# Maxima ahead of the scores in masked attention steps, by quarters of the array, with cleared queries for rows that see no key

## The chip, the cores and the metric

The kernel runs on one core of a Trainium2 chip. The metric is the device time of one execution in microseconds (us), as the median of several runs. PE is the core's matrix engine (TensorE), PEld its weight loads, DVE the vector engine, ACT the scalar engine, POOL is GpSimd, and SP the engine whose queue issues nearly all DMAs. PSUM is the memory that PE's matmuls write, SBUF the other on-chip memory.

## The reference, cut to what matters

Two transformer layers are computed on 2048 rows of width 256, with 16 heads of width 16. The first layer holds a self attention and a cross attention between the two halves of the rows, the second a masked self attention and a cross attention to 1601 context rows; each layer ends in an MLP. That makes four attention stages, numbered 0 to 3 in the kernel. Stage 2 is the masked one:

```python
scores = jnp.einsum('bhqd,bhkd->bhqk', q, k) / jnp.sqrt(jnp.float32(hd))
if mask is not None:
    scores = jnp.where(mask == 0, jnp.float32(-1000000000.0), scores)
attn = jax.nn.softmax(scores, axis=-1)
out = jnp.einsum('bhqk,bhkd->bhqd', attn, v)
```

The mask is a full 2048 by 2048 array of integers, the same for all heads, and the kernel must take any such array. In a row whose keys are all masked, all scores are the same number, so that the softmax is even over all keys.

## The kernel before

**Units and steps.** The rows are worked on in four blocks of 512 queries (`BLK`), the heads in four groups of four (`g`). A unit is one stage, one block and one group. Within a unit a step handles 128 keys for two heads (`i` picks the pair, `h` the head within it): a PSUM tile `s_ps` of 128 keys by 2 x 512 queries. The keys of a stage lie in two slots of 1024. The first masked block (`SPLIT`) is worked on one slot at a time, as part 0 and part 1, because the keys of the second slot are ready later: its eight units have 16 steps. The other three masked blocks have twelve units of 32 steps. That makes 512 masked steps.

**What a step does.** `weights_of` makes the exponentials of one step (PE to PSUM, then one ACT instruction, L1251), transposed, with keys on partitions. In masked stages four matmuls of 64 by 64 first bring in the mask (L1224: an identity times a transposed part of the mask, `bias_columns`, 0 or -2^60). Each takes one quarter of the array: 64 rows (partitions read) by 64 columns (partitions written). Then come two matmuls of scores (L1241, fp32 operands of 64 rows by 128 columns, one for each head), and last two matmuls that subtract each query's maximum (`less_maxima`, L1232, bf16: `sel` holds ones in the rows of `nm` that belong to the head). In unmasked stages the maxima come first and the scores last. A step also does one tile of the next unit's maxima: `maxima` computes scores the other way round (L1142, and L1136 where a head's keys are written in two halves), and DVE reduces them (L1149 for masked tiles, which adds the mask from `bias_rows` too; L1156 for others). And it does a step of the value product of the unit, `values_of` (L1268, four column groups of 32).

**How maxima travel.** When the last tile of a unit's maxima is issued, four steps before the unit's own first step, `all_maxima` calls `negated` (L1170, L1173: three DVE instructions split each negated maximum into three bf16 parts in `maxpad`), and three steps later `as_rows` turns them with four matmuls (L1182) and an ACT copy (L1187) into the rows `nm`. Where a unit is a part, `as_rows` also sends rows of `nm` through twelve DMAs (L1194), by which the two parts are joined later.

**The mask.** `mask_rows` loads 128 queries by 512 keys of the mask (L1043, tile `raw`, two buffers) and POOL turns them into 0 or -2^60 in bf16 (L1044). For the second to fourth masked block this happens while the maxima of the group before (`g` = 3 of the block before) are computed, and `mask_columns` transposes them on PE (L1067) with an ACT copy (L1072).

**What sets the order.** Every engine's instructions stand in the order in which the Python code issues them. `stream` walks through the steps; lists of work with due steps (`later`), generators of background work (projections, norms, the next stage's keys and queries; L113 is their matmuls' line, L404 to L413 a norm) and a list of DMAs (`transfers`) are drawn on at each step. The three `s_ps` buffers are handed round between maxima tiles and exponential tiles; a query tile `q` has three buffers and is loaded two units ahead (L1010). POOL also scales each unit's output by its inverse sums (`divide`, L1344), which waits for a DMA.

Of the kernel before, what the change touches and what calls it, by code (L numbers as in the profile page):

```python
# [22 lines left out]
P = 128  # L23
# [7 lines left out]
BLK = 512  # L31
NB = S // BLK
TPB = BLK // P
# [3 lines left out]
MASKED = -float(2**60)  # L37
# [3 lines left out]
NPART = 3  # L41
# [6 lines left out]
SLOT = S // 2  # L48
# [6 lines left out]
SPLIT = ORDER[2][0]  # L55
# [3 lines left out]
AHEAD = 4  # L59
SPACING = 0.75  # L60
COLUMNS = 6


def key_rows(st, n):
# [3 lines left out]
def slot_rows(st, slot):  # L68
    return sum(key_rows(st, n) for n in KEYS[st][slot])
# [8 lines left out]
def two_layers(ctx: ExitStack, tc: tile.TileContext, a: dict, out: bass.AP):  # L78
    nc = tc.nc

    def pool(name, bufs=1, **kw):
        return ctx.enter_context(tc.tile_pool(name=name, bufs=bufs, **kw))
# [7 lines left out]
    sb = pool("sb")  # L90
# [24 lines left out]
    def big_ps(dtype=F32):  # L115
        flush((None,))
        return ps.tile([P, 2, BLK], dtype, tag="s", bufs=3, name="s_ps")

    def one_ps(dtype=F32, n=None):
        n = small[0] if n is None else n  # L120
        flush((n,))
        return ps.tile([P, BLK], dtype, tag=f"m{n}", bufs=1, name=f"m{n}_ps")
# [37 lines left out]
    ident = identR.bitcast(F32)  # L160
    ident16 = sb.tile([P, P], BF16, tag="ident16", name="ident16")
# [1 line left out]
    minus_half = sb.tile([P, TPB], F32, tag="minus_half", name="minus_half")  # L163
    nc.gpsimd.memset(minus_half, -0.5)

    maxpad = sb.tile([P, TPB, P], F32, tag="maxpad", name="maxpad")
    nc.gpsimd.memset(maxpad, 0.0)

    def upper(t):

        return t.bitcast(BF16).rearrange("... (x two) -> ... x two", two=2)[..., 1]

    sel = sb.tile([P, 2, P], BF16, tag="sel", name="sel")
    for i in range(2):
        col = sb.tile([P, 1], F32, tag=f"col{i}", name="col")
        v = ident.rearrange("p (c x) -> p c x", c=2)[:, :, i : 2 * NPART : 2]
        nc.vector.tensor_reduce(col, v, AX.XY, ALU.add)
        nc.vector.tensor_copy(sel[:, i, :], col.to_broadcast([P, P]))

    kT: list = [[None, None] for _ in range(NG)]  # L180
    V: list = [[None, None] for _ in range(NG)]
# [19 lines left out]
    def half(shape, dtype=F32, name="half"):  # L201
        return sb.tile(shape, dtype, tag="half", bufs=3, name=name)
# [822 lines left out]
    def mask_rows(b, slot, qt, j):  # L1025

        if (b, slot, qt) not in bias_rows:
            if b != SPLIT:
                t = sb.tile([P, 2, SLOT], BF16, tag="w_mlp", bufs=WB, name="bias")
                for s in range(2):  # L1030
                    bias_rows[b, s, qt] = t[:, s, :]
            elif slot == 0:

                t = sb.tile([P, TPB, SLOT], BF16, tag="kT11", name="bias")
                for q in range(TPB):
                    bias_rows[b, slot, q] = t[:, q, :]
            else:
                t = sb.tile([P, 2, SLOT], BF16, tag="w_mlp", bufs=WB, name="bias")
                for q2 in range(2):
                    bias_rows[b, slot, qt + q2] = t[:, q2, :]  # L1040
        raw = sb.tile([P, BLK], I32, tag="raw", bufs=2, name="raw")
        q0, k0 = b * BLK + qt * P, KEYS[2][slot][j] * BLK
        nc.sync.dma_start(raw, a["mask"][q0 : q0 + P, k0 : k0 + BLK])  # L1043
        nc.gpsimd.tensor_scalar(  # L1044
            bias_rows[b, slot, qt][:, j * BLK : (j + 1) * BLK], raw, 0.0, MASKED,
            ALU.is_equal, ALU.mult,
        )

    def mask_part(slot):

        for n in range(2 * TPB):
            later.append([n, lambda n=n: mask_rows(SPLIT, slot, n // 2, n % 2), False])
# [112 lines left out]

    def negated(u):

        v = maxpad.rearrange("p t (c x) -> p t c x", c=2)
        high = upper(maxpad).rearrange("p t (c x) -> p t c x", c=2)
        nc.vector.tensor_reduce(v[:, :, :, :2], u["pm"], AX.X, ALU.max, negate=True)  # L1170
        for n in range(NPART - 1):
            at = slice(2 * n, 2 * n + 2)
            nc.vector.tensor_tensor(  # L1173
                v[:, :, :, 2 * n + 2 : 2 * n + 4], v[:, :, :, at], high[:, :, :, at], ALU.subtract
            )

    def as_rows(u):

        m = one_ps()
        high = upper(maxpad)  # L1180
        for qt in range(TPB):
            nc.tensor.matmul(  # L1182
                m[:, qt * P : (qt + 1) * P], lhsT=high[:, qt, :], rhs=ident16,
                start=True, stop=True,
            )
        u["nm"] = sb.tile([P, BLK], BF16, tag="nm", bufs=2, name="nm")
        nc.scalar.copy(u["nm"], m)  # L1187
        if "part" in u:

            t = sb.tile([P, NPART, 4 * BLK // P], BF16, tag="mh", bufs=2, name="mh")  # L1190
            for j in range(4):
                for h in range(NPART):
                    r = 64 * (j // 2) + 2 * h + j % 2
                    nc.sync.dma_start(  # L1194
                        t[PH * j : PH * (j + 1), h, :], u["nm"][r : r + 1, :]
                    )

            def add():
                n = u["minus"] = part_tile(u, "minus")
                nc.vector.tensor_tensor(n, t[:, 0, :], t[:, 1, :], ALU.add)  # L1200
                for h in range(2, NPART):
                    nc.vector.tensor_tensor(n, n, t[:, h, :], ALU.add)

            later.append([4, add, False])

    def part_tile(u, name):
        return sb.tile([P, 4 * BLK // P], F32, tag=f"{name}{u['g']}{u['part']}", name=name)

    def weights_of(u):

        st, b, g = u["st"], u["b"], u["g"]
        masked = st == 2
        u["tiles"] = [
            (slot, kt, min(P, slot_rows(st, slot) - kt * P))
            for slot in u["slots"] for kt in range(-(-slot_rows(st, slot) // P))
        ]
        u["e"] = {}

        def pair(n, i):
            slot, kt, r = u["tiles"][n]  # L1220
            s = big_ps()
            for h, half_ in ((0, 0), (0, 1), (1, 0), (1, 1)) if masked else ():
                to, of = 64 * half_, 64 * (half_ ^ h)
                nc.tensor.matmul(  # L1224
                    s[to : to + 64, h, :],
                    lhsT=ident16[of : of + 64, of : of + 64],
                    rhs=bias_columns[b, slot, kt][of : of + 64, :],
                    start=True, stop=False,
                )
            def less_maxima():  # L1230
                for h in range(2):
                    nc.tensor.matmul(  # L1232
                        s[:r, h, :],
                        lhsT=sel[64 * h : 64 * h + 64, i, :r],
                        rhs=u["nm"][64 * h : 64 * h + 64, :],
                        start=not masked, stop=masked,
                    )

            def scores():
                for h in range(2):  # L1240
                    nc.tensor.matmul(  # L1241
                        s[:r, h, :],
                        lhsT=kT[g][slot][64 * h : 64 * h + 64, i, kt * P : kt * P + r],
                        rhs=u["q"][64 * h : 64 * h + 64, i, :],
                        start=False, stop=not masked,
                    )

            for f in (scores, less_maxima) if masked else (less_maxima, scores):
                f()
            e = u["e"][n, i] = sb.tile([P, 2, BLK], F32, tag="e", bufs=EB, name="e")  # L1250
            nc.scalar.activation(e[:r], s[:r], AF.Exp, scale=SCALE)  # L1251

        return [lambda n=n, i=i: pair(n, i) for n in range(len(u["tiles"])) for i in range(2)]
# [157 lines left out]
    def stream(stages, start_up):  # L1411
# [19 lines left out]
        at = 0  # L1431
        for u in units:
            steps = [(slot, kt) for slot in u["slots"] for kt in range(-(-slot_rows(u["st"], slot) // P))]
            if u["st"] == 2 and u["g"] == 0:
                columns += [
                    (at + 2 * n - COLUMNS, u["b"], slot, kt) for n, (slot, kt) in enumerate(steps)
                ]
# [20 lines left out]
                    all_maxima(u)  # L1458

        def all_maxima(u):  # L1460
            negated(u)
            later.append([3, lambda: as_rows(u), True])
            if u.get("part") == 0 and u["g"] == NG - 1:
                want(2, 1, 1)
# [38 lines left out]
        for u in units:  # L1503
            i = u["i"]
            masked = u["st"] == 2
            small[0] = i % 2
            second = weights_of(u)
            for s2 in range(len(second)):
# [10 lines left out]
                f = pending.pop(0) if pending else None  # L1519
# [12 lines left out]
                if s2 == 2 and i:  # L1532
# [6 lines left out]
                    elif part == 1:  # L1539
                        v = units[i - 1 - NG]  # L1540
# [143 lines left out]
```

## Time and profile before

| what | value |
|---|---|
| median of 3 runs | 3057.54 us (3054.51 to 3059.77) |
| the profiled execution's own time | 3064.13 us |
| its span in the profile | 3062.4 us |
| mean granted PE clock | 0.971 |
| busy: PE, DVE, ACT, POOL | 2826.0, 2174.5, 1721.8, 388.9 us |
| first to last mask matmul (L1224) | 1129.3 to 2266.9 us |
| L1251, the exponentials | 1440 of 1024 ns |
| L1149, the masked maxima | 1024 of 700 ns |

Times in the profile are of one execution. Each row of a view gives a line of the kernel, its engine, the operation, `out<-in` by the program's names, and the shape; for matmuls a shape such as 64*128 says how many rows and columns of the array it takes. In the timeline instructions of one kind that follow each other are one row; its first number is the start, its second the length. What stands in brackets is how long the engine was idle before the row and what ended that; `issue` there means that no other engine was waited for. The ends of matmuls are modelled, so that two starts tell more than a length. The chain of waits is followed back from the last instruction; its shares say which line's work stood on the path that set the end.

### The profile page before, as it was taken

How to read it: one execution, taken by the hardware profiler on the slowest of the kernel's cores; microseconds unless marked ns; L12 is line 12 of the kernel's file. 1: busy time of each engine (PE TensorE's matmuls, PEld its weight loads, DVE VectorE, ACT ScalarE, POOL GpSimd, SP SyncE). 2: the span in 40 equal slices, each digit the busy share in tenths (PEclk: the TensorE clock that was granted, in tenths of full speed). 3: DMA queues.
4: the chain of work that ended last, by engine and by line, in shares of the span. 5: the costliest groups of instructions: out<-in, count | busy, mean ns of one | idle time of the engine just before them, and what ended most of it. 6: DMA issues, size and time to landing. Idle time of an engine off the chain costs nothing.

```text
span 3062.4 us, 71795 instructions
## 1 busy us (share of the span) xinstructions
PE 2826.0 (92%) x30040; PEld 1258.6 (41%) x30040; DVE 2174.5 (71%) x3856; ACT 1721.8 (56%) x1897; POOL 388.9 (13%) x333
## 2 busy tenths in 40 slices
PE   6999999989998999786999999999999999999997
PEld 2334433333343344333444444444434444444442
DVE  5777777766766577465878878877768858858562
ACT  1466666665655556343555565565556746657472
POOL 0001101101010210203212101301001011110110
PEclk8999999999999999898999999999999999999998
DMA  7652262261205321443212001102242000100000
GB/s 220 143 97 92 67 109 66 75 115 34 73 28 110 60 78 42 108 92 104 68 31 65 29 21 53 55 19 60 46 68 84 24 21 27 28 21 23 21 22 12
DMA packets 178640, 192.11 MB, mean 63 GB/s; under 512 B 95476, under 2 KB 112380, under 8 KB 178316
## 3 DMA queue, kind: packets, MB, share of 16 engines
q1 hardware_dynamic: 177164, 187.52, 24.7%
q8 instruction: 236, 3.87, 0.6%
q14 instruction: 88, 0.72, 0.1%
q10 hardware_dynamic: 1152, 0.00, 0.0%
HBM read 129.78 MB, written 48.45 MB: 58 GB/s over the span
## 4 chain that ended last, share of the span: by engine, by line
PE 73%; DVE 9%; DMA 8%; SPq 4%; ACT 3%; issue 2%; POOL 1%; DVEq 0%; ACTq 0%; POOLq 0%
PE m_ps L1268 20%; PE m_ps L113 12%; PE s_ps L1241 11%; PE s_ps L1232 11%; PE s_ps L1142 8%; PE s_ps L1224 5%; DVE pm L1156 3%; DVE s_ps L1149 2%; PE s_ps L1136 2%; ACT e L1251 1%; DMA rd_dr<-rd 1%; DMA kT<-k_dr 1%; PE s_ps L113 1%; SPq L1194 1%; DVE t L413 1%
## 5 line engine op out<-in xcount | busy, mean ns | idle before, releaser
L1251 ACT ACTIVATE e<-s_ps 128x1024 f32<-128x1024 f32 (+1 forms) x1440 | 1474.0, 1024 | 1054.6 <-PE s_ps L1241 570.0
L1156 DVE TENSOR_REDUCE pm<-s_ps 128x2 f32<-128x1024 f32 x896 | 1090.6, 1224 | 315.2 <-PE s_ps L1142 300.3
L1268 PE MATMUL m_ps<-e,V 128*32 128x256 f32 (+1 forms) x11520 | 928.9, 393 | 11.8 <-DVE lo L496 11.6
L1149 DVE CUSTOM_DVE_ANT_0 s_ps<-s_ps,bias 128x512 f32<-128x512 f32 x1024 | 713.2, 700 | 211.2 <-PE s_ps L1136 191.0
L1241 PE MATMUL s_ps<-q,kT 64*128 64x512 f32 (+1 forms) x2880 | 805.5, 555 | 0.0
L1142 PE MATMUL s_ps<-kT,q 64*128 64x512 f32 (+2 forms) x2560 | 689.0, 436 | 45.9 <-DMA kT<-k_dr 19.3
L1232 PE MATMUL s_ps<-nm,sel 64*128 64x512 bf16 (+1 forms) x2880 | 567.9, 391 | 40.7 <-DVE pm L1156 28.9
L1268 PEld LDWEIGHTS m_ps<-e,V 128*32 128x32 f32 (+1 forms) x11520 | 250.2, 109 | 339.6 <-issue 236.1
L1142 PEld LDWEIGHTS s_ps<-kT,q 64*128 64x128 f32 x2560 | 295.9, 190 | 190.2 <-ACT e L1251 124.6
L1232 PEld LDWEIGHTS <-sel 64*128 64x128 bf16 (+1 forms) x2880 | 144.7, 93 | 506.2 <-issue 470.3
L1241 PEld LDWEIGHTS s_ps<-q,kT 64*128 64x128 f32 (+1 forms) x2880 | 281.6, 192 | 117.2 <-issue 117.2
L1136 PE MATMUL s_ps<-kT,q 64*128 64x256 f32 x1024 | 291.2, 366 | 3.5 <-DMA kT<-k_dr 2.7
L1344 POOL TENSOR_TENSOR oT<-oT,rd_rows 64x512 f32<-64x512 f32 x63 | 80.1, 1271 | 1592.3 <-DMA rd_rows<-rd_dr 1304.7
L1224 PE MATMUL s_ps<-biasT,ident 64*64 64x512 bf16 x2048 | 210.8, 402 | 9.8 <-DVE pm L1149 7.9
L1136 PEld LDWEIGHTS s_ps<-kT,q 64*128 64x128 f32 x1024 | 194.3, 193 | 18.2 <-DMA kT<-k_dr 3.2
L1044 POOL TENSOR_SCALAR bias<-raw 128x512 bf16<-128x512 int32 x64 | 123.0, 1922 | 274.6 <-DMA raw<-in_mask 258.2
L1224 PEld LDWEIGHTS <-ident 64*64 64x64 bf16 x2048 | 58.5, 103 | 223.7 <-issue 188.1
L1149 DVE DVE_READ_ACCUMULATOR2_ANT pm<- 128x1 f32 x1024 | 144.9, 142 | 0.0
L113 PE MATMUL m_ps<-hT,w_qk 128*32 128x512 f32 (+2 forms) x928 | 112.8, 604 | 12.8 <-DVE lo L496 10.2
L496 DVE SCALAR_TENSOR_TENSOR lo<-m_ps,qkb,hi 128x512 fp32r<-128x512 f32 (+3 forms) x62 | 43.5, 701 | 113.7 <-ACT hi L495 55.6
L113 PE MATMUL m_ps<-w_mlp,hid 128*32 128x256 f32 x1792 | 105.2, 388 | 11.2 <-ACT sums L1298 11.2
L113 PE MATMUL m_ps<-hT,w_mlp 128*32 128x512 f32 x896 | 107.7, 598 | 7.3 <-ACT sums L1298 4.3
(123 smaller groups left out, 1334.7 us busy)
## 6 DMA issues: line engine op xcount, KB each, us to landing
q<-q_dr SPq DMA_DIRECT2D x544, 64.0 KB
kT<-k_dr SPq DMA_DIRECT2D x192, 128.0 KB
raw<-in_mask SPq DMA_DIRECT2D x64, 256.0 KB
oT<-sums SPq DMA_DIRECT2D x256, 32.0 KB
rd_rows<-rd_dr SPq DMA_DIRECT2D x63, 128.0 KB
q_dr<-hi SPq DMA_DIRECT2D x30, 256.0 KB
q_dr<-lo SPq DMA_DIRECT2D x30, 256.0 KB
k_dr<-hi SPq DMA_DIRECT2D x24, 256.0 KB
```

What stands on the lines that cost most here:

```text
L113: nc.tensor.matmul(m[at:to], lhsT=lhsT[:, at:to], rhs=rhs, start=start, stop=stop)
L1044: nc.gpsimd.tensor_scalar(bias_rows[b, slot, qt][:, j * BLK : (j + 1) * BLK], raw, 0.0, MASKED, ALU.is_equal, ALU.mult,)
L1136: nc.tensor.matmul(exchanged(s[:, h, :], part), lhsT=queries(qt, h, i), rhs=exchanged(keys(slot, c, x, h, i), 1 - part), start=True, stop= ...
L1142: nc.tensor.matmul(s[:, h, at : at + x], lhsT=queries(qt, h, i), rhs=keys(slot, c, x, h, i), start=True, stop=True,)
L1149: nc.vector.tensor_tensor_reduce(out=s[:, h, :], in0=s[:, h, :], in1=bias_rows[b, slot, qt][:, c : c + BLK], scale=1.0, scalar=-3.0e38, op ...
L1156: nc.vector.tensor_reduce(u["pm"][:, qt, :, i, n], s, AX.X, ALU.max)
L1224: nc.tensor.matmul(s[to : to + 64, h, :], lhsT=ident16[of : of + 64, of : of + 64], rhs=bias_columns[b, slot, kt][of : of + 64, :], start= ...
L1232: nc.tensor.matmul(s[:r, h, :], lhsT=sel[64 * h : 64 * h + 64, i, :r], rhs=u["nm"][64 * h : 64 * h + 64, :], start=not masked, stop=masked,)
L1241: nc.tensor.matmul(s[:r, h, :], lhsT=kT[g][slot][64 * h : 64 * h + 64, i, kt * P : kt * P + r], rhs=u["q"][64 * h : 64 * h + 64, i, :], st ...
L1251: nc.scalar.activation(e[:r], s[:r], AF.Exp, scale=SCALE)
L1268: nc.tensor.matmul(u["av"][PH * j : PH * (j + 1), cut], lhsT=V[g][slot][:r, kt * GW + j * VW : kt * GW + j * VW + PH], rhs=u["e"][n, j % 2 ...
L1344: nc.gpsimd.tensor_tensor(v, v, u["rd"], ALU.mult)
```

## The change

Four things are changed.

- In masked steps the maxima are subtracted before the scores, directly after the mask, and by four matmuls of 64 by 64 instead of two of 64 by 128. `sel` and the columns of `maxpad` are laid out anew, and `as_rows` writes the maxima of both heads to both halves of `nm`, by eight matmuls with 64 columns instead of four with 128.
- With a mask of -2^60 ahead and the maximum of a row without any visible key taken away again before its scores are added, these scores would no longer vanish in the rounding. So the queries of such rows are set to zero: `clear_rows` multiplies the query tile by 0 or 1 on POOL, in place, when all maxima tiles of a masked unit have been issued.
- Which rows these are is found on the chip: `sum_rows` lets ACT copy each finished tile of `bias_rows` (128 queries by 1024 keys) onto itself with a sum over the keys, six steps (`SUMS`) after the row's second half was asked for.
- `flag_rows`, two steps after a block's last sum (five times in all, the block `SPLIT` having a flag for each part), compares the sums on DVE, turns the flags with four matmuls and copies them on ACT.

```diff
-    maxpad = sb.tile([P, TPB, P], F32, tag="maxpad", name="maxpad")
+    maxpad = sb.tile([P, TPB, P // 2], F32, tag="maxpad", name="maxpad")
...
-    sel = sb.tile([P, 2, P], BF16, tag="sel", name="sel")
-    for i in range(2):
...
+    sel = sb.tile([P, 2, 2, P], BF16, tag="sel", name="sel")
+    for h in range(2):
+        for i in range(2):
+            col = sb.tile([P, 1], F32, tag=f"col{h}{i}", name="col")
+            at = 8 * h + i
+            v = ident.rearrange("p (c x) -> p c x", c=2)[:, :, at : at + 2 * NPART : 2]
+            nc.vector.tensor_reduce(col, v, AX.XY, ALU.add)
+            nc.vector.tensor_copy(sel[:, h, i, :], col.to_broadcast([P, P]))
...
+        if j == 1:
+            later.append([SUMS, lambda: sum_rows(b, slot, qt), False])
...
+    def sum_rows(b, slot, qt):
+        key = (b, slots_together(b, slot))
...
+        t = bias_rows[b, slot, qt]
+        nc.scalar.activation(
+            t, t, AF.Copy, accum_out=masked_sums[key][:, qt, slot : slot + 1]
+        )
+        if qt == TPB - 1 and slot == key[1][-1]:
+            later.append([2, lambda: flag_rows(*key), True])
+
+    def flag_rows(b, slots):
+        total = sb.tile([P, TPB], F32, tag="rd", bufs=4, name="total")
+        nc.vector.tensor_reduce(
+            total, masked_sums[b, slots][:, :, slots[0] : slots[-1] + 1], AX.X, ALU.add
+        )
+        cut = MASKED * (SLOT * len(slots) - 0.5)
+        flag = half([P, TPB, P], BF16, name="flag")
+        nc.vector.tensor_scalar(
+            flag, total.unsqueeze(2).to_broadcast([P, TPB, P]), cut, None, ALU.is_gt
+        )
+        m = one_ps()
+        for qt in range(TPB):
+            nc.tensor.matmul(
+                m[:, qt * P : (qt + 1) * P], lhsT=flag[:, qt, :], rhs=ident16,
+                start=True, stop=True,
+            )
+        t = row_flags[b, slots] = sb.tile([P, BLK], BF16, tag="flags", bufs=2, name="flags")
+        nc.scalar.copy(t, m)
+
+    def clear_rows(u):
+        t = row_flags[u["b"], tuple(u["slots"])]
+        q = u["q"]
+        nc.gpsimd.tensor_tensor(q, q.bitcast(F32), t.unsqueeze(1).to_broadcast([P, 2, BLK]), ALU.mult)
...
         for qt in range(TPB):
-            nc.tensor.matmul(
-                m[:, qt * P : (qt + 1) * P], lhsT=high[:, qt, :], rhs=ident16,
-                start=True, stop=True,
-            )
+            for c in range(2):
+                nc.tensor.matmul(
+                    m[64 * c : 64 * c + 64, qt * P : (qt + 1) * P], lhsT=high[:, qt, :],
+                    rhs=ident16, start=True, stop=True,
+                )
...
             def less_maxima():
-                for h in range(2):
+                for h, half_ in ((0, 0), (0, 1), (1, 0), (1, 1)) if masked else ():
+                    to = slice(64 * half_, 64 * half_ + 64)
+                    of = slice(64 * (half_ ^ h), 64 * (half_ ^ h) + 64)
+                    nc.tensor.matmul(
+                        s[to, h, :], lhsT=sel[of, h, i, to], rhs=u["nm"][of, :],
+                        start=False, stop=False,
+                    )
+                for h in () if masked else range(2):
...
-            for f in (scores, less_maxima) if masked else (less_maxima, scores):
-                f()
+            less_maxima()
+            scores()
...
         def all_maxima(u):
+            if u["st"] == 2:
+                clear_rows(u)
             negated(u)
```

More of the change, by code (lines that the diff above doesn't have):

```diff
@@ L61 @@
 COLUMNS = 6
+SUMS = 6
 def key_rows(st, n):
@@ L171, in upper @@
         return t.bitcast(BF16).rearrange("... (x two) -> ... x two", two=2)[..., 1]
-    sel = sb.tile([P, 2, P], BF16, tag="sel", name="sel")
-    for i in range(2):
[L175 to L178, printed above, removed]
+    sel = sb.tile([P, 2, 2, P], BF16, tag="sel", name="sel")
[6 more added lines that the diff above has]
+            nc.vector.tensor_copy(sel[:, h, i, :], col.to_broadcast([P, P]))
     kT: list = [[None, None] for _ in range(NG)]
@@ L1047, in mask_rows, with slots_together @@
         )
+        if j == 1:
+            later.append([SUMS, lambda: sum_rows(b, slot, qt), False])
+    masked_sums: dict = {}
+    row_flags: dict = {}
+    def slots_together(b, slot):
+        return (slot,) if b == SPLIT else (0, 1)
+    def sum_rows(b, slot, qt):
+        key = (b, slots_together(b, slot))
+        if key not in masked_sums:
+            masked_sums[key] = sb.tile([P, TPB, 2], F32, tag="masked_sums", bufs=2, name="masked_sums")
+        t = bias_rows[b, slot, qt]
[26 more added lines that the diff above has]
+        nc.gpsimd.tensor_tensor(q, q.bitcast(F32), t.unsqueeze(1).to_broadcast([P, 2, BLK]), ALU.mult)
     def mask_part(slot):
@@ L1166, in negated @@
     def negated(u):
-        v = maxpad.rearrange("p t (c x) -> p t c x", c=2)
-        high = upper(maxpad).rearrange("p t (c x) -> p t c x", c=2)
+        v = maxpad[:, :, :16].rearrange("p t (h x) -> p t h x", h=2)
+        high = upper(maxpad)[:, :, :16].rearrange("p t (h x) -> p t h x", h=2)
         nc.vector.tensor_reduce(v[:, :, :, :2], u["pm"], AX.X, ALU.max, negate=True)
@@ L1192, in as_rows @@
                 for h in range(NPART):
-                    r = 64 * (j // 2) + 2 * h + j % 2
+                    r = 8 * (j // 2) + 2 * h + j % 2
                     nc.sync.dma_start(
@@ L1230, in less_maxima @@
             def less_maxima():
-                for h in range(2):
+                for h, half_ in ((0, 0), (0, 1), (1, 0), (1, 1)) if masked else ():
[6 more added lines that the diff above has]
+                for h in () if masked else range(2):
                     nc.tensor.matmul(
                         s[:r, h, :],
-                        lhsT=sel[64 * h : 64 * h + 64, i, :r],
+                        lhsT=sel[64 * h : 64 * h + 64, h, i, :r],
                         rhs=u["nm"][64 * h : 64 * h + 64, :],
-                        start=not masked, stop=masked,
+                        start=True, stop=False,
                     )
@@ L1244, in scores @@
                         rhs=u["q"][64 * h : 64 * h + 64, i, :],
-                        start=False, stop=not masked,
+                        start=False, stop=True,
                     )
-            for f in (scores, less_maxima) if masked else (less_maxima, scores):
-                f()
+            less_maxima()
+            scores()
             e = u["e"][n, i] = sb.tile([P, 2, BLK], F32, tag="e", bufs=EB, name="e")
```

## The prediction

> **What bounds the kernel now.** I read the page's chain first, then the chain of each of the two stretches that hold masked steps, then single steps in the timeline.
>
> The page's chain by engine:
>
> ```profile
> PE 73%; DVE 9%; DMA 8%; SPq 4%; ACT 3%; issue 2%; POOL 1%; DVEq 0%; ACTq 0%; POOLq 0%
> ```
>
> The chain by line from 1510 us to 2267 us (twelve masked units of 32 steps), then from 1129 us to 1510 us (eight units of 16 steps):
>
> ```profile
> by line: PE m_ps L1268 27.0%; PE s_ps L1241 20.8%; PE s_ps L1224 16.6%; PE s_ps L1232 11.3%; PE s_ps L1142 6.0%; PE s_ps L1136 5.1%; DVE s_ps L1149 3.2%; PE m_ps L113 3.0%; PE m_ps L1067 2.0%; issue 1.0%; DVE t L413 0.9%; ACT e L1251 0.8%;
> ...
> by line: PE m_ps L113 13.3%; PE m_ps L1268 8.8%; DVE s_ps L1149 8.4%; PE s_ps L1241 7.6%; SPq L1194 7.6%; PE s_ps L1224 6.2%; issue 4.5%; PE s_ps L1232 4.2%; DMA c<-in_ctx 3.3%; PE s_ps L1136 2.5%; DMA raw<-in_mask 2.4%; PE s_ps L1142 2.2%;
> ```
>
> In the first stretch PE's lines add up to 92%, in the second to 45%; the rest there is SP's issues, DMAs and DVE. So a microsecond of PE is worth 0.92 us in the 384 steps of the one and about 0.45 us in the 128 of the other: 384 x 0.92 + 128 x 0.45 = 411 steps' worth.
>
> One masked step, PE in the timeline (start, length, line):
>
> ```profile
> 1701.05 0.41 PE L1224 MATMUL s_ps<-biasT,ident 64*64 64x512 bf16 x4
> 1701.39 0.50 PE L1241 MATMUL s_ps<-q,kT 64*128 64x512 f32 x2
> 1701.73 0.39 PE L1232 MATMUL s_ps<-nm,sel 64*128 64x512 bf16 x2
> 1701.77 0.57 PE L1142 MATMUL s_ps<-kT,q 64*128 64x512 f32 x1
> 1701.78 0.58 PE L1136 MATMUL s_ps<-kT,q 64*128 64x256 f32 x2
> 1702.29 0.64 PE L1268 MATMUL m_ps<-e,V 128*32 128x256 f32 x8
> 1702.86 0.41 PE L1224 MATMUL s_ps<-biasT,ident 64*64 64x512 bf16 x4
> ```
>
> and its weight loads:
>
> ```profile
> 1701.39 0.19 PEld L1241 LDWEIGHTS s_ps<-q,kT 64*128 64x128 f32 x2 [0.23 <-issue]
> 1701.73 0.10 PEld L1232 LDWEIGHTS <-sel 64*128 64x128 bf16 x2 [0.15 <-issue]
> 1701.73 0.20 PEld L1142 LDWEIGHTS s_ps<-kT,q 64*128 64x128 f32 x1
> 1701.74 0.41 PEld L1136 LDWEIGHTS s_ps<-kT,q 64*128 64x128 f32 x2
> ```
>
> The step is 1.81 us: mask to scores 0.34, scores to maxima 0.34, maxima with the next unit's scores to the value product 0.56, value product 0.57. Mark what stands behind the loads. L1232's weights were loaded only when the scores had run, 0.34 us after them; L1142's, with the same tile shape and rows, were loaded at once, at 1701.73, under L1232's matmuls. So fp32 after bf16 flows on; bf16 after fp32 stops and starts anew. The unmasked step, which already has maxima ahead of scores, agrees:
>
> ```profile
> 802.73 0.39 PE L1232 MATMUL s_ps<-nm,sel 64*128 64x512 bf16 x2
> 802.77 0.58 PE L1241 MATMUL s_ps<-q,kT 64*128 64x512 f32 x2
> 803.19 0.40 PE L1142 MATMUL s_ps<-kT,q 64*128 64x512 f32 x2
> 803.52 0.64 PE L1268 MATMUL m_ps<-e,V 128*32 128x256 f32 x8
> ```
>
> **The step's own gain.** Three groups there take 0.79 us up to the value product, two in the masked step take 0.56: one more group that flows on costs 0.23 us, against 0.34 for one that stops. The change puts the maxima, now 64*64 like the mask, directly behind the mask: bf16 after bf16, same shape. Mask 0.34, maxima 0.21 to 0.24 on top, scores and next scores 0.56, values 0.57. The saving is 0.34 less 0.21 to 0.24, so 0.10 to 0.13; I take 0.115, the step becomes 1.69 us, and 411 x 0.115 = 47 us (43 to 52). That there are four matmuls for two costs no stream time if the four quarters run together, as L1224's four do, started within 0.01 us and done with in 0.34. No row shows a second set of 64*64 weights loaded under a first; the nearest is L1268, whose second four 128*32 loads start 0.03 us after the first four and whose second matmuls follow 0.24 us after the first. I take that side; the other end is a full stop of 0.34, no saving.
>
> [...]
>
> **What it adds.** First, the wait for nm. Maxima were the third thing of a step and become the second; PE's matmuls of scores and all behind them now queue behind it. At a unit's start:
>
> ```profile
> 1707.64 1.02 ACT L1251 ACTIVATE e<-s_ps 128x1024 f32<-128x1024 f32 x1 [0.78 <-PE s_ps L1232]
> 1708.56 0.58 ACT L1187 CAST nm<-m_ps 128x512 bf16<-128x512 f32 x1
> 1709.78 1.02 ACT L1251 ACTIVATE e<-s_ps 128x1024 f32<-128x1024 f32 x1 [0.63 <-PE s_ps L1232]
> ```
>
> nm is done at 1709.14, behind an exponential; mask starts at 1708.61, and L1232 had until 1709.29. Now it is wanted at 1708.85 or, as the exponential too moves forward, 0.4 to 0.5 us before nm is there. 0.45 us x (12 x 0.92 + 8 x 0.45 = 14.6) = 7 us; between 0 and 0.6 each, 9.
>
> Second, 32 ACT copies with sums, 128x1024 in bf16; nearest row the exponential of the same size, 1.02 us. They wait for POOL's L1044; set against the trace of before, each would come 5.7 us or more after its row of mask, so ACT does not stand. But ACT has 0.78 us idle a step, about 0.66 after, so an exponential ends some 0.4 us late, its PSUM buffer is free late, and PE's next L1142 has about 0.25 us to spare: 0.2 to 0.3 us lost each. 16 lie in the long stretch: 4 us; the other 16 where other things bind: 3. Bounds 0 and 32 x 1.02 = 33.
>
> Third, five flags: a DVE pair, four matmuls like L1182's (0.33 us up to the next work), an ACT copy of 0.58: 0.6 us each, 3 us; bounds 1.6 and 10. Fourth, the 68 transposes of maxima become eight half-wide matmuls: nothing if halves run together like L1268's columns, 0.22 us each (15 in all) if not; I take 2.
>
> Fifth, 20 multiplications of q on POOL, 128x1024. L1344's 64x512 took 1.27, so 2.54 us. Scores wait for them, and everything behind scores on PE. Cover: the last maxima tile is done when DVE starts L1170, at 1704.10, and that unit's mask starts at 1710.41. The multiplication starts about 1.6 us sooner than L1170 and has 6 us and more; I take nothing, 51 us if all cover is gone. On POOL it is put past others: in the third unit of a block, mask rows that ran at 1617 to 1624 now stand behind a multiplication at about 1645, and SP's third load of raw with them; but SP's next, L1010, waited for PE until 1651.46 anyway, and the first row's sum comes 42 us after its row. At 1256 us four rows of mask stand ahead of one multiplication; it ends near 1258.6, and the unit starts at 1261.05.
>
> Sixth, DVE. Two L1149 with their reads take 1.44 us where they run back to back, against a step of 1.69 instead of 1.81. Its other work in a block of 128 steps is about 11 us, against 32 us to spare: not the bound, but what a norm (L404, L413: 4 us) holds up is recovered over more steps: 3 us.
>
> Sum: 7 + 7 + 3 + 2 + 0 + 3 = 22. 47 - 22 = 25 us. The profiled execution took 3064.13 us (span 3062.4), 0.2% over the median of 3057.54; 3064.1 - 25 = 3039, and at the median's level 3032.5 us. Under 0.2% (6 us) this measurement cannot tell from no change.
>
> **Rivals.** (1) As above, 0.66: 3032, own range 3012 to 3046. (2) The step gains, and the adds eat it: ACT's sums and nm at their upper ends (26 us more would do for zero; 15 to 20 are likelier): about 3050, from 3046 to 3062; 0.14, more than half of it faster. For it: 16 sums in an otherwise even stretch. Against: ACT's idle 0.78. (3) The second quarters stop as scores to maxima did: no saving, 22 us of adds, 3079; 0.13. It decides from a mask-to-maxima interval of 0.34 - 22/411 = 0.29 us upward. For it: no row shows two sets of quarters. Against: L1268's second loads. (4) POOL late with q, 8 us of PE wait a block over what I count: 3065 with the spread around it; 0.07. It decides where POOL's queue ends over 5 us after the maxima. That the change does not do what it says has no room: the order of PE's instructions is written out.
>
> Faster: 0.66 + 0.08 = 0.74. Same: 0.06 + 0.03 = 0.09. Slower: 0.13 + 0.04 = 0.17. The range leaves out (3) above and the last 0.06 below: 3010 to 3066.
>
> **What would show it.** Right: L1224's line to L1232's in 0.21 to 0.24 us with no idle before the second loads, steps of 1.69 us, nm the only wait at a unit's start, 0.4 to 0.5 us, twenty times. Wrong: an interval of 0.3 or more there; steps that follow DVE's rhythm of 1.5 to 1.6 us and leave PE idle; PE waiting for POOL's q; more than 0.3 us lost at each sum. The whole is wrong if the masked stretch from first to last mask matmul (1137.6 us) does not shrink by 15 to 40 us.

## The result, and the profile after

The changed kernel takes 3079.56 us in the median (six runs, 3074.45 to 3089.94), the kernel before 3063.0 us beside it (six runs, 3054.51 to 3068.29). The ratio is 1.0051, interval 1.0034 to 1.0067: slower by 16 us where 25 us of gain were forecast, and outside the forecast range. The profiled execution took 3081.63 us with a span of 3079.5, against 3064.13 and 3062.4. All of the 17 us lie between the first and the last mask matmul: 1154.9 us, before 1137.6.

The page's chain by engine is the same as before but for two points of DMA and one of SP, and the chain by line over the twelve long units (1520 to 2282 us) has 91% in PE's lines, where it had 92%:

```profile
PE 73%; DVE 9%; DMA 6%; SPq 5%; ACT 3%; issue 2%; POOL 1%; DVEq 0%; ACTq 0%; POOLq 0%
```

```profile
by line: PE m_ps L1325 27.0%; PE s_ps L1298 20.8%; PE s_ps L1274 16.6%; PE s_ps L1284 10.6%; PE s_ps L1191 6.0%; PE s_ps L1185 5.1%; PE m_ps L114 3.0%; DVE s_ps L1198 3.0%; PE m_ps L1116 2.0%; issue 1.2%; ACT e L1308 0.9%; DVE t L416 0.9%; 
```

So PE is the bound as it was. Line numbers are those of the kernel that ran, so the same work has other numbers from run to run. One masked step in PE's timeline (L1274 mask, L1284 maxima, L1298 scores, L1191 and L1185 the next unit's scores, L1325 values):

```profile
1701.51 0.41 PE L1274 MATMUL s_ps<-biasT,ident 64*64 64x512 bf16 x4
1701.75 0.39 PE L1284 MATMUL s_ps<-nm,sel 64*64 64x512 bf16 x4
1702.07 0.51 PE L1298 MATMUL s_ps<-q,kT 64*128 64x512 f32 x2
1702.41 0.39 PE L1191 MATMUL s_ps<-kT,q 64*128 64x512 f32 x1
1702.41 0.40 PE L1185 MATMUL s_ps<-kT,q 64*128 64x256 f32 x2
1702.74 0.64 PE L1325 MATMUL m_ps<-e,V 128*32 128x256 f32 x8
1703.31 0.41 PE L1274 MATMUL s_ps<-biasT,ident 64*64 64x512 bf16 x4
```

and the weight loads of that step:

```profile
1701.51 0.11 PEld L1274 LDWEIGHTS <-ident 64*64 64x64 bf16 x4 [0.41 <-issue]
1701.54 0.12 PEld L1284 LDWEIGHTS <-sel 64*64 64x64 bf16 x4
1702.07 0.19 PEld L1298 LDWEIGHTS s_ps<-q,kT 64*128 64x128 f32 x2 [0.41 <-issue]
1702.17 0.19 PEld L1191 LDWEIGHTS s_ps<-kT,q 64*128 64x128 f32 x1
```

Mask to maxima is 0.24 us, as forecast: the second quarters' weights are loaded 0.03 us after the first, with no idle time. But the step is 1.80 us (median of the long units 1.788; before 1.806). What the maxima gave, the scores took: 0.32 from maxima to scores, 0.34 from scores to the next unit's scores, 0.33 on to the values. The forecast had 0.56 for the last two together (scores to the next unit's scores, and on to the values); they take 0.67.

The second finding is at each of the five flags. DVE and PE around the fourth:

```profile
1724.20 0.39 PE L1185 MATMUL s_ps<-kT,q 64*128 64x256 f32 x2
1724.74 0.70 DVE L1198 CUSTOM_DVE_ANT_0 s_ps<-s_ps,bias 128x512 f32<-128x512 f32 x1 [0.20 <-PE s_ps L1185]
...
1725.54 0.70 DVE L1198 CUSTOM_DVE_ANT_0 s_ps<-s_ps,bias 128x512 f32<-128x512 f32 x1
...
1726.15 0.16 DVE L1075 TENSOR_REDUCE total<-masked_sums 128x4 f32<-128x8 f32 x1
1726.34 0.43 DVE L1080 TENSOR_SCALAR flag<-total 128x512 bf16<-128x512 f32 x1
1726.83 0.40 PE L1085 MATMUL m_ps<-ident,flag 128*128 128x128 bf16 x4 [2.24 <-DVE flag L1080]
```

and PE in windows of 1 us (length, PE busy, granted clock, DMA share, GB/s):

```profile
1727.00:1728.00 1.00, 1.00 (x20) 1.00 0.08 12
1728.00:1729.00 1.00, 1.00 (x12) 0.58 0.24 55
1729.00:1730.00 1.00, 1.00 (x13) 0.50 0.26 55
1730.00:1731.00 1.00, 1.00 (x16) 0.50 0.04 10
1731.00:1732.00 1.00, 1.00 (x13) 0.72 0.00 0
1732.00:1733.00 1.00, 1.00 (x20) 1.00 0.00 0
```

In the order in which the code issues them, PE's four matmuls (L1085) follow directly on DVE's comparison (L1080). But DVE still has a step's maxima tiles in front of it, the first of which waited for PE until 1724.74 us. The values' matmuls (L1325), next in PE's order, start behind the four at 1727.15 us, and PE does nothing for 2.24 us; and when it works again, its clock is granted at half for about 3.4 us (1728.2 to 1731.6, worked out from the windows' 0.58 and 0.72 with 0.50 as the low value). The three steps from 1723 us on are 2.6, 1.0 and 0.5 us longer than in order_alone below, which has no flags: 4.1 us for what was forecast at 0.6. (Mask matmuls start at 1723.31, 1727.72, 1730.51 and 1732.75 us here, and at 1712.29, 1714.08, 1715.87 and 1717.65 in order_alone.) The low clock does not follow on every stop of this length: in halves_ahead below the same flag stopped PE for 2.24 us as well, the clock stayed at 1.00 in every window up to 1731 us, and only one step was longer, 4.33 us instead of 1.70 (behind it mask matmuls start at 1727.38, 1729.08 and 1730.78 us).

### The profile page after: what moved, and what is told of

Read it like the earlier page. It is cut to its first block, busy times and chain, and to the rows that moved or that the text cites. A ratio compares the mean times of both kernels' runs of the same rounds, so it can differ in the third digit from the quotient of the medians.

```text
span 3079.5 us, 74565 instructions
## 1 busy us (share of the span) xinstructions
PE 2843.0 (92%) x31356; PEld 1235.5 (40%) x31356; DVE 2183.0 (71%) x3870; ACT 1756.7 (57%) x1966; POOL 431.6 (14%) x353
## 4 chain that ended last, share of the span: by engine, by line
PE 73%; DVE 9%; DMA 6%; SPq 5%; ACT 3%; issue 2%; POOL 1%; DVEq 0%; ACTq 0%; POOLq 0%
PE m_ps L1325 20%; PE m_ps L114 13%; PE s_ps L1298 11%; PE s_ps L1191 8%; PE s_ps L1289 7%; PE s_ps L1274 5%; PE s_ps L1284 3%; DVE pm L1205 2%; DVE s_ps L1198 2%; PE s_ps L1185 2%; PE s_ps L114 1%; ACT e L1308 1%; DMA rd_dr<-rd 1%; DMA kT<-k_dr 1%; SPq L1244 1%
## 5 line engine op out<-in xcount | busy, mean ns | idle before, releaser
L1325 PE MATMUL m_ps<-e,V 128*32 128x256 f32 (+1 forms) x11520 | 935.7, 395 | 12.1 <-DVE lo L499 11.9
L1198 DVE CUSTOM_DVE_ANT_0 s_ps<-s_ps,bias 128x512 f32<-128x512 f32 x1024 | 713.5, 701 | 229.0 <-PE s_ps L1185 205.0
L1298 PE MATMUL s_ps<-q,kT 64*128 64x512 f32 (+1 forms) x2880 | 810.4, 559 | 0.0
L1191 PE MATMUL s_ps<-kT,q 64*128 64x512 f32 (+2 forms) x2560 | 599.1, 400 | 45.3 <-DMA kT<-k_dr 19.0
L1289 PE MATMUL s_ps<-nm,sel 64*128 64x512 bf16 (+1 forms) x1856 | 367.9, 392 | 33.5 <-DVE pm L1205 21.6
L1325 PEld LDWEIGHTS m_ps<-e,V 128*32 128x32 f32 (+1 forms) x11520 | 251.0, 109 | 342.6 <-issue 241.7
L1298 PEld LDWEIGHTS s_ps<-q,kT 64*128 64x128 f32 (+1 forms) x2880 | 282.6, 193 | 215.4 <-issue 215.4
L1191 PEld LDWEIGHTS s_ps<-kT,q 64*128 64x128 f32 x2560 | 291.5, 188 | 188.6 <-ACT e L1308 125.5
L1289 PEld LDWEIGHTS <-sel 64*128 64x128 bf16 (+1 forms) x1856 | 95.1, 93 | 423.5 <-issue 418.6
L1274 PE MATMUL s_ps<-biasT,ident 64*64 64x512 bf16 x2048 | 212.7, 405 | 11.7 <-DVE pm L1198 9.8
L1185 PE MATMUL s_ps<-kT,q 64*128 64x256 f32 x1024 | 205.2, 282 | 3.2 <-DMA kT<-k_dr 3.1
L1185 PEld LDWEIGHTS s_ps<-kT,q 64*128 64x128 f32 x1024 | 191.0, 190 | 26.1 <-issue 4.0
L1284 PE MATMUL s_ps<-nm,sel 64*64 64x512 bf16 x2048 | 200.9, 382 | 0.2 <-ACT nm L1237 0.2
L1274 PEld LDWEIGHTS <-ident 64*64 64x64 bf16 x2048 | 58.4, 103 | 229.2 <-issue 188.6
L1198 DVE DVE_READ_ACCUMULATOR2_ANT pm<- 128x1 f32 x1024 | 145.0, 142 | 0.0
```

What stands on the lines that cost most here:

```text
L1185: nc.tensor.matmul(exchanged(s[:, h, :], part), lhsT=queries(qt, h, i), rhs=exchanged(keys(slot, c, x, h, i), 1 - part), start=True, stop= ...
L1191: nc.tensor.matmul(s[:, h, at : at + x], lhsT=queries(qt, h, i), rhs=keys(slot, c, x, h, i), start=True, stop=True,)
L1198: nc.vector.tensor_tensor_reduce(out=s[:, h, :], in0=s[:, h, :], in1=bias_rows[b, slot, qt][:, c : c + BLK], scale=1.0, scalar=-3.0e38, op ...
L1274: nc.tensor.matmul(s[to : to + 64, h, :], lhsT=ident16[of : of + 64, of : of + 64], rhs=bias_columns[b, slot, kt][of : of + 64, :], start= ...
L1284: nc.tensor.matmul(s[to, h, :], lhsT=sel[of, h, i, to], rhs=u["nm"][of, :], start=False, stop=False,)
L1289: nc.tensor.matmul(s[:r, h, :], lhsT=sel[64 * h : 64 * h + 64, h, i, :r], rhs=u["nm"][64 * h : 64 * h + 64, :], start=True, stop=False,)
```

## The experiments

Each ratio is to the kernel before in runs on the same chip, five rounds, with a 95% interval. Not all kernels ran on the same chip, so two of them are compared by their ratios, not by their times. "Stretch" is the time from first to last mask matmul in the profiled execution (before 1137.6, after 1154.9 us), "step" the median masked step of the long units (before 1.806, after 1.788).

| kernel | ratio, interval | stretch | step |
|---|---|---|---|
| adds_order_before | 1.0074, 1.0054 to 1.0094 | 1162.1 | 1.806 |
| order_alone | 0.9967, 0.9953 to 0.9981 | 1135.6 | 1.787 |
| flags_later | 1.0010, 0.9999 to 1.0021 | 1145.2 | 1.788 |
| halves_ahead | 0.9931, 0.9918 to 0.9944 | 1116.1 | 1.697 |
| halves_flags_later | 0.9904, 0.9887 to 0.9921 | 1110.2 | 1.697 |
| halves_alone | 0.9851, 0.9829 to 0.9873 | 1095.7 | 1.697 |
| order_sums | 0.9980, 0.9966 to 0.9993 | 1132.1 | 1.787 |
| order_clear | 0.9991, 0.9976 to 1.0006 | 1136.2 | 1.788 |
| halves_no_flags | 0.9879, 0.9864 to 0.9895 | 1104.4 | 1.697 |
| halves_flags_pool | 0.9885, 0.9868 to 0.9903 | 1107.2 | 1.697 |
| scores_bf16 | 0.9927, 0.9910 to 0.9944 | 1124.4 | 1.695 |

**The adds without the order.** Everything that the change adds stays; in masked steps the scores come first again and the maxima last, as two matmuls of 64 by 128.

```diff
-            less_maxima()      # four quarters
-            scores()
+            for f in (scores, less_maxima) if masked else (less_maxima, scores):
+                f()            # less_maxima: two halves
```

> Sums, flags, cleared queries and the new layout of sel and nm stay; in masked steps the scores come before the maxima again, and the maxima are two matmuls of 64*128 again. Theory A (the loss is the flags: PE stands about 2.2 us at each flag for DVE, and its clock is then low for some microseconds, 4 us each, four of them in the masked stretch): step 1.81 us as before, the flags cost the same as in the changed kernel, +16 to +22 us against before. Theory B (the loss is the new order: nm wanted earlier at each unit's start, and a step that gains nothing): 0 to +6 us.

The ratio says 23 us of cost, 3092.83 us against 3068.42, just over the upper end of theory A. The forecast's sum of adds, 22 us, looks right in size, but 7 of it were for nm being wanted sooner, which this order does not do: without them the forecast was 15.

**The order without the adds.** No sums, no flags, no clearing; a masked key counts -2^14 instead of -2^60, so that rows without a visible key are not treated.

```diff
-MASKED = -float(2**60)
+MASKED = -float(2**14)
-        if j == 1:
-            later.append([SUMS, lambda: sum_rows(b, slot, qt), False])
-            if u["st"] == 2:
-                clear_rows(u)
```

> Mask, maxima by quarters, scores, as in the changed kernel, but no sums, no flags and no clearing of queries; the mask's constant is -2^14 instead of -2^60, so that rows that see no key keep their own scores, which is not what the reference wants of them. Theory A: the step is 1.79 us instead of 1.81, some 350 steps that PE bounds, so -3 to -9 us against before. Theory B: +8 to +16 us.

The order alone gives 10 us by the ratio (2 in the stretch), not 47, and its step is that of the changed kernel. So the gain was never there to be eaten: the step's price was wrong. Against the changed kernel (1.0051) the adds cost 0.84% of 3065, 26 us; by the two stretches they cost 19.

**Maxima ahead, but as halves.** The changed kernel with the masked maxima as two matmuls of 64 by 128 ahead of the scores.

```diff
-                for h, half_ in ((0, 0), (0, 1), (1, 0), (1, 1)) if masked else ():
...
-                        s[to, h, :], lhsT=sel[of, h, i, to], rhs=u["nm"][of, :],
-                        start=False, stop=False,
+                for h in range(2):
+                    nc.tensor.matmul(
+                        s[:r, h, :], lhsT=sel[64 * h : 64 * h + 64, h, i, :r],
+                        rhs=u["nm"][64 * h : 64 * h + 64, :], start=not masked, stop=False,
+                    )
```

> The changed kernel, but the maxima of masked steps, still ahead of the scores, are two matmuls of 64*128 (halves, as in unmasked steps) instead of four of 64*64. Theory L (what a step loses is the load of fp32 weights that cannot go on ahead over a change of the tile shape; a bf16 group of the new shape in front hides it): mask 0.34, maxima with scores and next scores 0.79 as in the unmasked step, values 0.57, step 1.70 us, -0.1 us in some 350 steps; with the flags as in the changed kernel -18 to -28 us against before. [...]

Now the step is 1.697 us and the run 37 us below the changed kernel (1.0051 less 0.9931), 21 below the kernel before, as theory L had it. One step in PE's timeline (L1282 maxima, L1291 scores, L1318 values) and its weight loads show where the quarters lose:

```profile
1727.38 0.41 PE L1274 MATMUL s_ps<-biasT,ident 64*64 64x512 bf16 x4
1727.72 0.39 PE L1282 MATMUL s_ps<-nm,sel 64*128 64x512 bf16 x2
1727.76 0.58 PE L1291 MATMUL s_ps<-q,kT 64*128 64x512 f32 x2
1728.18 0.39 PE L1191 MATMUL s_ps<-kT,q 64*128 64x512 f32 x1
1728.51 0.64 PE L1318 MATMUL m_ps<-e,V 128*32 128x256 f32 x8
...
1727.72 0.10 PEld L1282 LDWEIGHTS <-sel 64*128 64x128 bf16 x2 [0.23 <-issue]
1727.72 0.20 PEld L1291 LDWEIGHTS s_ps<-q,kT 64*128 64x128 f32 x2
1727.95 0.19 PEld L1191 LDWEIGHTS s_ps<-kT,q 64*128 64x128 f32 x1
```

Mask (1727.38) to maxima is 0.34 here, 0.10 more than with quarters. But the load that stands first after the change of tile shape is now bf16 and takes 0.10 us, and the scores' fp32 load goes with it; three groups reach the values in 0.79 us (1728.51), and with the values' 0.57 that is 1.70. In the changed kernel the first load after the change of shape is the scores' own fp32 one of 0.19, and the next waits for it: 0.24 + 0.32 + 0.34 + 0.33 + 0.57 = 1.80.

**The same with nothing added.** Halves ahead, and the cuts of order_alone.

> Halves ahead of the scores without sums, flags and clearing, with the mask's constant of -2^14 (rows that see no key keep their own scores). Theory A+L: order_alone was -0.33% and halves for quarters gained 1.2% more, so -1.4 to -1.7%, -43 to -52 us. Rival (DVE the bound from 1.70 us on): -30 to -38 us.

The ratio gives 46 us (39 to 52) for the order by halves alone, very near the 47 that the forecast had for quarters, and DVE did not become the bound: the step stays at 1.697. That the two numbers meet is chance: the forecast's 0.115 us a step came from another account, as the next section shows.

**Quarters, with scores in bf16.** The direct trial of the load: the changed kernel, with masked scores computed from the upper halves of `kT` and `q`.

```diff
-                        lhsT=kT[g][slot][64 * h : 64 * h + 64, i, kt * P : kt * P + r],
-                        rhs=u["q"][64 * h : 64 * h + 64, i, :],
+                        lhsT=upper(kT[g][slot][64 * h : 64 * h + 64, i, kt * P : kt * P + r]),
+                        rhs=upper(u["q"][64 * h : 64 * h + 64, i, :]),
```

> The changed kernel, but in masked steps the scores take the upper bf16 halves of kT and q, so that their weights are bf16 with 128 columns; values and all maxima stay fp32. Scores are thereby rounded. Theory L (what a step pays behind the 64*64 groups is the fp32 weight load of the scores, which is not issued ahead over the change of tile shape: 0.19 us for fp32, 0.10 us for bf16): maxima to scores stays near 0.31, scores to the next unit's scores falls from 0.34 to about 0.24, so a step of 1.69 to 1.71 instead of 1.79, and the run is 30 to 40 us under the changed kernel, ratio 0.992 to 0.995 of before. Rival T (a change of shape costs the same whatever is loaded, and the halves were faster for another reason): step 1.78 to 1.80, ratio 1.003 to 1.007. Rival S (the bf16 views, every second element, stream slower): step over 1.80, slower than the changed kernel.

The loads of one step, of which the first stands behind the quarters, the second is the next unit's:

```profile
1700.78 0.10 PEld L1301 LDWEIGHTS <-kT 64*128 64x128 bf16 x2 [0.41 <-issue]
1700.79 0.20 PEld L1191 LDWEIGHTS s_ps<-kT,q 64*128 64x128 f32 x1
1700.79 0.42 PEld L1185 LDWEIGHTS s_ps<-kT,q 64*128 64x128 f32 x2
1701.35 0.16 PEld L1328 LDWEIGHTS m_ps<-e,V 128*32 128x32 f32 x8
```

The idle time of 0.41 before the scores' load stays, so the change of shape costs what it did. But the next unit's loads start 0.01 us later instead of 0.10, scores to values is 0.56 us instead of 0.67, and the step 1.695. In time that is 38 us under the changed kernel (1.0051 less 0.9927), as expected. One detail was not: the next unit's scores start 0.04 us after the scores (1700.79 to 1700.83), where theory L had about 0.24, and most of what they gain there they wait before the values; only the sum of the two intervals is as expected. This run settles that the scores' format is what the step paid for. It changes the loads and the streamed operand together. That it is the load and not the stream of fp32 is argued, not tried by itself: it rests on the load rows (0.10 against 0.19) and on halves_ahead, where the scores stream in fp32 as before, stand second, and the step is as short.

**The flags' matmuls three steps later.** The flag gets a tile of its own, DVE's two instructions stay where they are, and PE's four matmuls follow three steps on.

```diff
-        flag = half([P, TPB, P], BF16, name="flag")
+        flag = sb.tile([P, TPB, P], BF16, tag="flag", name="flag")
...
+        later.append([3, lambda: turn_flags(b, slots, flag), True])   # the four matmuls, the copy
```

> The changed kernel, with one edit: the four matmuls of a flag are issued three steps after its two DVE instructions instead of directly behind them (the flag has a tile of its own). Theory A: PE no longer waits at the flags and keeps its clock, 14 to 17 us less than the changed kernel, -3 to +3 us against before. Theory B: as the changed kernel, +13 to +18 us. A third reading, that the sums on ACT cost the time and the flags only show it: less than 5 us gained.

The stops at the flags are gone (no idle time before their matmuls) and the step is unchanged. The stretch is 10 us shorter than the changed kernel's and the run 13 us faster (1.0051 less 1.0010), a little less than theory A had. But a new wait of 4 us appears near 1500 us, where ACT's part of a projection (L498) waits for a DMA that SP issued behind eight others, and PE behind it loses 6 us in one step.

**Both edits.** Halves ahead and the flags' matmuls later, the whole computation:

> Halves ahead of the scores, and the flags' matmuls three steps after their DVE instructions: both edits in one kernel, with everything that the reference wants. Theory A+L (the step's gain and the flags' wait add up): halves_ahead was -0.69%, flags_later gained 0.41% on the changed kernel, so -1.0 to -1.25%, -30 to -38 us against before. Rival (with a step of 1.70 us DVE has become the bound, and what PE no longer waits for flags it waits for DVE): -20 to -26 us.

0.9904: faster than the kernel before by 30 us, the near end of theory A+L, and than halves_ahead by 8 (give or take 7). The wait near 1500 us is there too, 3.6 us long. To find whether the flag's own tile makes it, by changing which buffer of `half` comes next, the flag was taken from `half` again:

```diff
-        flag = sb.tile([P, TPB, P], BF16, tag="flag", name="flag")
+        flag = half([P, TPB, P], BF16, name="flag")
```

> The whole computation, as halves_flags_later, but the flag tile is taken from the three buffers of `half` again, as in the changed kernel; the flag's matmuls stay three steps behind its DVE instructions. Theory B (the 4 to 6 us at step 117 come from the flag tile having a buffer of its own: the three buffers of `half` are then handed round in another order and a projection's half waits for a DMA that SP issues late): that wait goes, 3032 to 3036, ratio 0.988 to 0.989, stretch from first to last mask matmul about 5 us shorter than the 1110.2 of halves_flags_later. Rival (the wait comes from moving the flag's matmuls behind by three steps): it stays, 3037 to 3042.

The time fell where that theory put it, 0.9885, but the theory is wrong: the interval overlaps that of halves_flags_later, and ACT's waits between 1483 and 1503 us still hold it (total, times, longest):

```profile
ACT hi L498 <- DMA k_dr<-hi: 3.4, 1, 3.4
```

It comes with moving the flag's matmuls, not with their tile. Why SP is later there was not settled. Both versions compute all of the reference, are faster than both kernels, and can't be told from each other.

**What each add costs.** The sums put back on order_alone; the clearing put back there, with a tile of ones; and halves with both of these but no flags.

> order_alone with the 32 sums on ACT, but without flags and clearing (mask's constant -2^14). If each sum delays an exponential and that a tile of maxima, as the prediction had it (7 us): -0.05 to -0.2%, 3 to 8 us more than order_alone. If ACT's idle time hides them: as order_alone, -0.25 to -0.45%.

> order_alone with the 20 multiplications of q on POOL, by a constant tile of ones, without sums and flags (mask's constant -2^14). If they lie under the steps between the last maxima tile and the unit's start: as order_alone, -0.25 to -0.45%. If scores or what stands behind them on POOL and SP wait for them: 4 us or more above order_alone, -0.2% or less.

> Left out: the five flags (DVE comparison, four matmuls, copy); q is multiplied by a tile of ones, the sums are made and not read, and a masked key counts -2^14, so that rows without a visible key are not treated. Theory F (of the adds, the flags alone cost much: a stop of PE and some steps at a low clock, 13 to 16 us; sums and clearing together cost under 10): halves_alone was 3021.5 and halves_ahead 3048.1 against a kernel before at the same level, so this run lands at 3024 to 3033, ratio 0.986 to 0.989, and no step of the second to fourth masked block is longer by over 1 us than in halves_alone. Rival (sums and clearing are the larger part, the flags 5 us or less): 3043 to 3048, ratio 0.992 to 0.994.

The first two say little by themselves: 4 us (0.9980 less 0.9967) and 7 us (0.9991), with intervals of about 4 and 5 us on each ratio, and stretches no more than 1 us longer than order_alone's. The third separates the flags: halves_ahead less halves_no_flags is 0.52%, 16 us (give or take 6 by the two intervals), and 11.7 us in the stretch, as theory F had it; one step of the later blocks is 1.1 us longer than in halves_alone, where the theory allowed 1. Sums and clearing together are 0.28%, 9 us (give or take 8), and 8.7 us in the stretch.

## Why the prediction was wrong, point by point

**The step's gain: the step that failed.** The forecast took 0.34 us (scores to maxima) as the price of a bf16 group that follows an fp32 group, and let it go when the maxima moved. It got the new interval right (0.24). The failing term is "scores and next scores 0.56". That 0.56 was read from the two groups at the end of the old step, of which the first was bf16: a short load after which fp32 loads go ahead. Put behind quarters, the scores are the first group of their shape and their longer load is exposed; the two take 0.67. Nor was the 0.34 the maxima's own: in the changed kernel an fp32 group, the next unit's scores, stands in their place behind the scores and starts 0.34 us after them too. The wait belongs to the fp32 group that leads. So the maxima's going shortened the way from scores to values by 0.23 us (0.90, 1701.39 to 1702.29, became 0.67), and their coming lengthened the way from mask to scores by 0.22 (0.34 became 0.56). Of 0.115 us a step about 0.02 remained: 411 x 0.018 = 7 us, and 10 by order_alone's ratio, instead of 47. The row that said so was on the forecast's own page: in the unmasked step the bf16 maxima lead, the scores start 0.04 us behind them, and three groups take 0.79 us that take 0.90 in the masked step, where scores lead. The forecast used its 0.79 for the price of "one more group" and not for which group led; the 0.11 between the two is what halves ahead bring.

**Counting changes of tile shape.** Before and after, the rows of a masked step show three changes (128*32 to 64*64 to 64*128 to 128*32), and those of halves_ahead and scores_bf16 the same three; the steps are 1.806, 1.788, 1.697 and 1.695 us. So the number of changes does not give the step. Nor do the loads of a second set of weights wait here for the running matmuls on the same quarters: L1284's start 0.03 us after L1274's, whose matmuls take 0.41 us.

**nm: 7 us forecast, nothing measured.** The forecast set the unit's first mask at 1708.61, which is the last step of the unit before; two paragraphs on it had the right 1710.41. The unit's last maxima tile is issued at 1701.77, and from that step to the unit's first are five steps, not four. In the changed kernel nm is there 1.5 us before it is wanted (at a unit's start 1716.68 and 1718.18 us), and one of the 2048 matmuls of L1284 is the only one to have waited:

```profile
  ACT nm L1237: 0.2, 1
```

**Flags: 3 us forecast with a bound of 10, 12 to 16 measured.** The instructions were priced, the queue was not. DVE runs behind PE by a step's tiles, as its maxima tiles wait for PE (205 of the 229 us that it stood idle before L1198); a pair of DVE instructions with PE's matmuls next in order makes PE wait until DVE has caught up, 2.2 to 2.5 us at each of the five. The forecast asked what is queued behind the waiting instruction for nm and not here. The low clock that followed at the fourth and fifth (granted 0.50) was not foreseen.

**Sums, clearing, turned maxima, DVE: 7 + 0 + 2 + 3 us forecast.** A sum takes 1049 ns on ACT and 193 more to read the accumulator, a multiplication 2.14 us on POOL (2.54 forecast). The measured 9 us for sums and clearing (give or take 8) does not contradict 7. The turned maxima: their eight matmuls take 0.35 us from L1232 to the values at a unit's start (1715.24 to 1715.59), four took 0.33 before, so nothing. The 3 us for DVE no run measured by itself. The sum of all adds came out as 23 to 26 us by the ratios and 19 to 25 by the stretches, near the forecast 22, but made up of other parts: that it was near is luck.

**The rivals.** The time is that of rival (3), to the microsecond, and by luck: it set its 3079 us 22 us above a kernel before at 3057.54 us, and the kernel before came out at 3063.0, 16 us below the changed one. Its mechanism is refuted. It was to decide from a mask-to-maxima interval of 0.29 us upward, and the interval is 0.24. Little was saved because the next group paid. Rival (2), adds eating a gain, fails as order_alone has the small gain by itself; rival (4), POOL late with q, has no trace either: the page puts the idle time before L1298's 2880 matmuls at 0.0 us. The last line of the forecast, that all is wrong unless the stretch shrinks by 15 to 40 us, is the one that came true.

## What to carry to other kernels

When matmul groups are reordered, ask which group stands first after each change of tile shape: in the load rows above its weight load was not issued ahead (0.23 or 0.41 us idle before it), so put there the group with the shortest load (here bf16 maxima in the shape of the fp32 scores), and read a group's price only from a place where the same kind of group precedes it. An instruction pair in which one engine (here PE) waits for a lagging one (here DVE) costs the lag, 2.2 to 2.5 us at each of the five flags, not its own length, which was priced at 0.6; put a few steps between the two. (Here three steps took the wait away, and another of about 4 us came up elsewhere.) And a stop of PE costs more than its length when the clock falls after it: 4.1 us for the 2.24 at the fourth flag.

## What the runs showed of the hardware

- The first weight load behind the change from 64*64 to 64*128 is exposed (PEld idle for 0.23 or 0.41 us before it): 0.10 us in bf16, 0.19 in fp32, worth some 0.09 us a step (1.697 and 1.695 against 1.788). Behind a leading bf16 group of the same shape the fp32 load starts with that group's or 0.01 us later, and its matmuls 0.04 us later; behind a leading fp32 group the next fp32 load starts 0.10 us and its matmuls 0.34 us later.
- After 2.24 us without work at the fourth flag PE's granted clock fell to 0.50 about 1.3 us after it had work again and stayed there some 3.4 us (worked out from the windows above), though PE was busy throughout. It did not always do so: after the same stop of 2.24 us in halves_ahead the clock stayed at 1.00 in every window up to 1731 us.
- A sum taken with an ACT copy adds an instruction of its own, 193 ns, behind the 1049 ns of the copy (128x1024 in bf16).
